# Four transposes of TensorE replaced by one block transpose of VectorE and sixteen transfers within SBUF

## The chip, the cores and the metric

The kernel runs on one core of a Trainium2 chip. A core has TensorE (matmuls and, in a queue of its own, the loads of their weights), VectorE (called DVE in the profile), ScalarE (ACT), GpSimd (POOL), and SyncE (SP), which here only issues transfers. The transfers run on 16 DMA engines. The metric is the device time of one execution in microseconds, the median of some runs.

## The reference, cut to what matters

Four graph layers on x of 128 batches, 128 nodes and 256 features, each followed by a residual sum and a layer norm. The change lies in layer 2, which takes each node's features through three weight matrices and mixes the three results by the diagonal, the upper and the lower triangle of the adjacency matrix:

```python
def _L2_gnn_ref(x, W, adj, bias):
    adj_0 = jnp.diag(jnp.diagonal(adj))
    adj_1 = jnp.triu(adj, k=1)
    adj_2 = jnp.tril(adj, k=-1)
    h = jnp.einsum('bjf,kfo->kbjo', x, W)
    out = jnp.einsum('ij,bjo->bio', adj_0, h[0]) + jnp.einsum('ij,bjo->bio', adj_1, h[1]) + jnp.einsum('ij,bjo->bio', adj_2, h[2])
    return out + bias[None, None, :]
...
# --- layer 2 (adj_resnorm) ---
x = _layernorm(x + _L2_gnn_ref(x, L2_gnn_W, adj, L2_gnn_bias), axis=-1)
```

Layer 1 comes before it: three products with the weights W1, W2, W3, each mixed by the squared adjacency matrix, with a ReLU after the first two. All is float32.

## The kernel before

The 128 batches are handled as 32 quads of four. The loop is a software pipeline: iteration k runs layer 3 of quad a = k - 1, layer 1's end and layer 2 of quad c = k, layer 0's end and layer 1's beginning of quad b = k + 1, the softmax of quad e = k + 2 and the first products of quad g = k + 3. Each engine executes its instructions in the order in which the program writes them.

Many 2 by 2 block products use Strassen and Winograd's seven products instead of eight. The class `Seven` holds them as p1 to p7. Some land in one PSUM bank after each other, so that the intermediate results are read out between them:

```python
def p7(self):
    self.mm(self.y, "S3", "T3", False)
    self.k3 = self.part(self.y, 2)
    self.out(1, 1, self.z, self.k3)

def p4(self):
    self.mm(self.y, "A22", "T4", False)
    self.out(1, 0, self.y, None)

def p3(self):
    self.mm(self.z, "S4", "B22", False)
    self.out(0, 1, self.z, self.k2)
```

In layer 1's first product, `first_seven`, `out` is a sum on VectorE (if something kept is added) and a ReLU on ScalarE, and gives the blocks of h1. `mix2` multiplies the h1 of one node group with the squared adjacency:

```python
def out(row, col, bank, kept_):                    # in first_seven
    h1 = temp("h1")
    if kept_ is not None:
        nc.vector.tensor_add(h1, bank, kept_)
    nc.scalar.activation(h1, bank if kept_ is None else h1, AF.Relu)
    for t in range(2):
        for c in range(2):
            s.h1[2 * row + t, 2 * col + c] = h1[:, (2 * t + c) * P:(2 * t + c + 1) * P]
...
def mix2(k, i):
    pm = ps("pm2").rearrange("p (r c n) -> p r c n", r=2, n=N)
    for c in range(K1):
        nc.tensor.matmul(pm[:, c // 2, c % 2, :], quads[k].h1[i, c], wt_t, start=True, stop=True)
    return pm
```

Layer 2 of quad c is a generator that is advanced step by step between other work. `head(p)` transposes the features of batches 2p and 2p + 1 on TensorE and copies them out of PSUM on ScalarE; `products(p, ...)` forms the sums of a seven-product on VectorE:

```python
def layer2(k, b, room=None):
    s = quads[k]
    adc = adc_tile()
    g = [wk.tile([P, 2, 3 * D], F32, tag="ms", name="g", bufs=1) if room is None else room,
         adc[:, :6 * D].rearrange("p (t f) -> p t f", t=2)]
    ...
    def head(p):
        pt = ps("pt3").rearrange("p (t c n) -> p t c n", t=2, c=DC)
        for t in range(2):
            for c in range(DC):
                nc.tensor.transpose(pt[:, t, c, :], s.xr[:, 2 * p + t, c * P:(c + 1) * P], ident)
        xt = temp("x2t").rearrange("p (t c n) -> p t c n", t=2, c=DC)
        nc.scalar.copy(xt, pt)
        return xt
    ...
    x0 = head(0)
    yield
    u = products(0, x0)
    if b is not None:
        pm = {i: mix2(b, i) for i in (2, 0, 1)}
        x1 = head(1)
        mixed(b, 0, pm[0])
        mixed(b, 1, pm[1])
        pm[3] = mix2(b, 3)
    else:
        x1 = head(1)
    v = products(1, x1)
    ...
    run(u.p1, u.p2, u.p5, u.p6, v.p1, v.p2, u.p7, v.p5, v.p6, u.p4, u.p3, v.p7)
```

The end of an iteration, where the change sits:

```python
        if has_e:
            attention(e)
            scatter(e)                 # four indirect transfers, then the load of the attention weights
        rest = third(c, 2)
        mix1(b, 0)
        mix1(b, 2)
        third_mix(c, 0)
        next(rest)
        w = first_seven(b)
        third_norm(c, 0)               # layer norm of the first two batches of quad c
        next(rest)
        run(w.p1, w.p5, w.p2)
        next(rest)
        if has_g:
            score(g, 0)
            gather_last(g)
        w.p6()
        next(rest, None)
        w.p7()
        third_mix(c, 2)
        w.p4()
        w.p3()
        quads[c].layer2 = layer2(c, b)
        next(quads[c].layer2)          # head(0)
        third_norm(c, 2)               # layer norm of the last two batches of quad c
        next(quads[c].layer2)          # products(0), mix2, head(1), products(1), the products
```

`third_norm` is a square root on ScalarE and the normalisation on VectorE. The tile m2 of quad b, which `mixed` fills for the next product, has seven blocks (B11, B21, B22, T1, T2, T3, T4) of 512 elements a partition; its block T2 is written by `late_sums` at the start of the next iteration.

Of the kernel before, what the change touches and what calls it, by code (L numbers as in the profile page):

```python
# [8 lines left out]
F32 = mybir.dt.float32  # L9
# [17 lines left out]
def gnn_stack(ctx: ExitStack, tc: tile.TileContext, x, adj, w_qv_t, a, w_out_t, src, dst,  # L27
# [18 lines left out]
    P = 128  # L46
# [82 lines left out]
    with ExitStack() as phase:  # L129
# [306 lines left out]
        def scatter(k, load=True):  # L436
            s = quads[k]
            ad = att_dram[k % 2]
            for c in range(NE):
                nc.gpsimd.indirect_dma_start(out=ad, out_offset=bass.IndirectOffsetOnAxis(ap=att_idx[:, c:c + 1], axis=0),  # L440
                                             in_=s.at[:, c, :], in_offset=None)
            if load:
                load_weights(k)
# [54 lines left out]
        def mix1(k, j):  # L498
            s = quads[k]
            pm = ps("pm").rearrange("p (b c n) -> p b c n", b=2, c=DC)  # L500
            for t in range(2):
                for dc in range(DC):
                    nc.tensor.matmul(pm[:, t, dc, :], s.xr[:, j + t, dc * P:(dc + 1) * P], wt_t,
                                     start=True, stop=True)
            mx = temp("mx").rearrange("p (b c n) -> p b c n", b=2, c=DC)
            nc.scalar.copy(mx, pm)
            if j == 0:
                s.mx = {}
                s.h1 = {}
                s.m2 = m2_tile().rearrange("p (t c b n) -> p t c b n", t=7, c=2, b=2)  # L510
            s.mx[j] = mx
# [188 lines left out]
        def third_norm(k, j):  # L700
            s = quads[k]
            xj = s.xr[:, j:j + 2, :]
            norm_apply(wk, xj, s.mv, norm_root(wk, s.mv))
            if j == 0:
                s.xb = wk.tile([P, QB, D], F32, tag="xb", name=f"xb{k}", bufs=1)
            nc.gpsimd.tensor_add(s.xb[:, j:j + 2, :], xj, bias.unsqueeze(1).to_broadcast([P, 2, D]))  # L706

        def layer2(k, b, room=None):

            s = quads[k]
            adc = adc_tile()
            g = [wk.tile([P, 2, 3 * D], F32, tag="ms", name="g", bufs=1) if room is None else room,
                 adc[:, :6 * D].rearrange("p (t f) -> p t f", t=2)]
            sums = [adc[:, 6 * D:], None]
            half = 3 * D // 2
# [11 lines that stand above are left out]
            def products(p, xt):  # L729
                room = sums[p] if p == 0 else temp("x2s")  # L730
                a = {f"A{t + 1}{c + 1}": xt[:, t, c, :] for t in range(2) for c in range(DC)}
                for i in range(4):
                    a[f"S{i + 1}"] = room[:, i * N:(i + 1) * N]
                sums_a(a, a)
                keep = {}

                def mm(bank, i, j, new):
                    nc.tensor.matmul(bank[:, :half], a[i], layer2.blocks[j], start=new, stop=True,  # L738
                                     skip_group_check=True)

                def part(bank, i):
                    if i < 2:
                        keep[i] = temp("x2k")
                    to = keep[i % 2][:, :half]
                    nc.scalar.copy(to, bank[:, :half])  # L745
                    return to

                def out(row, col, bank, kept_):
                    to = g[p][:, row, col * half:(col + 1) * half]
                    if kept_ is None:  # L750
                        nc.scalar.copy(to, bank[:, :half])
                    else:
                        nc.vector.tensor_add(to, bank[:, :half], kept_)

                return Seven(mm, part, out)

            def scaled(p):
                xb = s.xb[:, 2 * p:2 * p + 2, :]
                nc.vector.scalar_tensor_tensor(xb, g[p][:, :, :D], diag_col, xb, op0=ALU.mult, op1=ALU.add)

            def mix(p):
                po = pos[p]
                for i in range(2):
                    nc.tensor.matmul(po, split_t[:, i, :], g[p][:, :, (i + 1) * D:(i + 2) * D],
                                     start=(i == 0), stop=(i == 1))
                return po

            def norm(p, po):
                xj = s.xr[:, 2 * p:2 * p + 2, :]
                nc.vector.tensor_add(xj, s.xb[:, 2 * p:2 * p + 2, :], po)  # L770
                return norm_stats(wk, xj)

            def normed(p, mv):
                norm_apply(wk, s.xr[:, 2 * p:2 * p + 2, :], mv, norm_root(wk, mv))

            x0 = head(0)
            yield
            u = products(0, x0)
            if b is not None:
# [10 lines that stand above are left out]
                mixed(b, 2, pm[2])  # L790
                mixed(b, 3, pm[3])
            run(u.p1, u.p2, u.p5, u.p6, v.p1, v.p2, u.p7, v.p5, v.p6, u.p4, u.p3, v.p7)
            pos = [ps("po2").rearrange("p (t d) -> p t d", d=D) for _ in range(2)]
            yield
            scaled(0)
            v.p4()
            yield
            v.p3()
            po = mix(0)
            scaled(1)  # L800
            yield
            mv = norm(0, po)
            yield
            po = mix(1)
            yield
            normed(0, mv)
            mv = norm(1, po)
            yield
            normed(1, mv)
            nc.sync.dma_start(x3_dram[k], s.xr.rearrange("p b d -> p (b d)"))  # L810
# [112 lines left out]
        def iteration(k):  # L923
# [100 lines left out]
                pass  # L1024
            if has_e:
                attention(e)
                scatter(e)
            rest = third(c, 2)
            mix1(b, 0)
            mix1(b, 2)  # L1030
# [1 line left out]
            next(rest)  # L1032
            w = first_seven(b)
            third_norm(c, 0)
            next(rest)
            run(w.p1, w.p5, w.p2)
            next(rest)
# [14 lines left out]
        def iteration_0():  # L1052

            late_sums(0)
            between = {i: [] for i in range(14)}
            for c, i in ((0, 0), (1, 3), (2, 6)):
                between[i].append(lambda c=c: score(2, c))
            between[2] += [lambda: attention(1), lambda: scatter(1)]
            between[3].append(lambda: gather_last(2))
            second(0, between)  # L1060
            small_loads()
            first_seven.blocks = weight_blocks(w1_sb, w1_s)
            layer2.blocks = weight_blocks(l2w, l2w_s)
            rest = third(0, 0)
            next(rest)
            score(2, NE - 1)
            gather(3)
            for j in range(QB):
                by_row(1, j)
            for _ in rest:  # L1070
                pass
            hidden_sums()
            aggregate(1)
            steps = softmax_parts(2)
            for _ in range(4):
                next(steps)
            stage_a(1)
            third_mix(0, 0)
            rest = third(0, 2)
            next(rest)  # L1080
            third_norm(0, 0)
            next(steps)
            mix1(1, 0)
            next(rest)
            mix1(1, 2)
            w = first_seven(1)
            next(rest)
            w.p1()
            for _ in steps:
                pass  # L1090
            run(w.p5, w.p2)
            next(rest, None)
            attention(2)
            scatter(2)
            w.p6()
            score(3, 0)
            gather_last(3)
            w.p7()
            third_mix(0, 2)
            w.p4()  # L1100
            w.p3()
            quads[0].layer2 = layer2(0, 1)
            next(quads[0].layer2)
            third_norm(0, 2)
            next(quads[0].layer2)
# [565 lines left out]
```

## Time and profile before

| | |
|---|---|
| time, median of 3 runs | 3103.06 us (3100.27 to 3104.02) |
| span of the profiled run | 3097.3 us |
| DMA engines, mean over the span | 109 GB/s of HBM traffic |
| transfers issued by SyncE | 495 |
| transposes of line 724 (`head`) | 256 in 64 calls, 39.6 us busy |

The profile is of one execution. PE is TensorE's matmuls, PEld its weight loads. A group of instructions is named by line, engine, operation, written and read tiles, shape and count; then come the busy time, the mean duration of one, and the idle time of the engine before them with what ended it. A timeline row has start and duration in us, engine, line, operation, tiles, shape and count. Matmuls are pipelined, so that their durations overlap; what one costs the stream is the distance from its start to the next start. L602 and L682 are layer 1's second and third product, L559 is `mix2`, L302 a seven-product of layer 0 or of layer 1's beginning, L738 one of layer 2.

### The profile page before, as it was taken

To read this page: it belongs to the slowest core of one execution; us is meant where nothing else is said; L and a number is where in the kernel's file an instruction comes from. 1 tells how busy PE (TensorE), PEld (TensorE's weight loads), DVE (VectorE), ACT (ScalarE), POOL (GpSimd) and SP (SyncE) were. 2 spreads that over 40 slices of the span, in tenths; PEclk is the share of its full clock that TensorE was granted. 3 is DMA by queue.
4 is the path that set the end of the run, shared out by engine and by line. 5 is a ranking of instruction groups with operands and counts; after the bars stand their busy time and mean duration, and the time that the engine had idled before them with its cause. 6 is when DMAs were issued, how large, how long until landed. Compare 5 with 4: busy or idle time off the path is not lost. (4 is left out here: it accounts for less than half of the span.)

```text
span 3097.3 us, 39721 instructions
## 1 busy us (share of the span) xinstructions
PE 3047.4 (98%) x14576; PEld 2382.0 (77%) x14576; DVE 2311.5 (75%) x4599; ACT 1388.0 (45%) x2547; POOL 652.6 (21%) x536
## 2 busy tenths in 40 slices
PE   8899999999999999999999999999999999999987
PEld 4688888888888888888888888888888887864444
DVE  8777777777777777777777777777777776457888
ACT  3344444344444444443344444444443344326668
POOL 3311112222222121122222211111122220001135
PEclk9999999999999999999999999999999999999999
DMA  5633333334333333333344433333343331015567
GB/s 183 162 103 95 77 97 110 103 103 110 110 103 93 99 103 88 84 103 108 98 110 110 110 96 90 109 95 75 98 110 103 103 110 42 21 44 201 172 206 261
DMA packets 220962, 340.06 MB, mean 110 GB/s; under 512 B 132704, under 2 KB 155104, under 8 KB 212448
## 3 DMA queue, kind: packets, MB, share of 16 engines
q0 software_dynamic: 44688, 148.40, 19.6%
q1 hardware_dynamic: 174320, 188.19, 18.5%
q8 instruction: 116, 1.90, 0.2%
q10 hardware_dynamic: 1760, 0.92, 0.1%
q14 instruction: 78, 0.64, 0.1%
HBM read 252.00 MB, written 85.46 MB: 109 GB/s over the span
## 5 line engine op out<-in xcount | busy, mean ns | idle before, releaser
L602 PE MATMUL ph<-m,w 128*128 128x256 f32 x2048 | 473.1, 379 | 0.0
L682 PE MATMUL p<-w,h 128*128 128x256 f32 x2048 | 462.8, 379 | 0.0
L602 PEld LDWEIGHTS ph<-m,w 128*128 128x128 f32 x2048 | 386.8, 190 | 79.9 <-issue 14.8
L682 PEld LDWEIGHTS p<-w,h 128*128 128x128 f32 x2048 | 388.9, 190 | 66.4 <-issue 7.9
L358 POOL DMA_INDIRECT zs<-qd,src_idx x120 | 116.3, 969 | 1330.2 <-DMA qd<-qt 1295.8
L602 PE MATMUL ph<-m,w_s 128*128 128x256 f32 x1536 | 357.7, 379 | 0.4 <-DVE h L614 0.4
L602 PEld LDWEIGHTS ph<-m,w_s 128*128 128x128 f32 x1536 | 291.7, 190 | 53.7 <-issue 14.8
L358 POOL DMA_INDIRECT zs<-qd,dst_idx x120 | 189.6, 1580 | 339.7 <-DMA zs<-qd,src_idx 330.2
L608 ACT COPY u<-ph 128x512 f32<-128x512 f32 x128 | 74.8, 584 | 354.9 <-PE ph L602 354.9
L440 POOL DMA_INDIRECT attd<-at,att_idx x128 | 142.8, 1116 | 342.3 <-DMA attd<-at,att_idx 251.0
L113 ACT ACTIVATE ln_sd<-ln_mv,eps 128x2 f32<-128x2 f32 x192 | 55.9, 291 | 276.4 <-DVE ln_mv L108 276.3
L618 ACT ACTIVATE h<-h 128x512 f32<-128x512 f32 x192 | 121.1, 631 | 87.2 <-DVE h L614 87.2
L390 DVE SCALAR_TENSOR_TENSOR zs<-zs 128x1024 f32<-128x1024 f32 x125 | 151.3, 1210 | 7.7 <-DMA zs<-qd,dst_idx 5.1
L392 DVE TENSOR_TENSOR zs<-zs,a_bc 128x1024 f32<-128x1024 f32 x125 | 153.2, 1225 | 4.3
L393 DVE TENSOR_REDUCE scores<-zs 128x16 f32<-128x1024 f32 x125 | 152.5, 1220 | 4.3
L745 ACT COPY x2k<-y 128x384 f32<-128x384 f32 x192 | 92.0, 479 | 139.5 <-PE y L738 114.2
L106 DVE BATCH_NORM_STATS2 ln_st<-xr 128x6 f32<-128x256 f32 x384 | 144.5, 418 | 6.6
L121 DVE TENSOR_SCALAR xr<-xr,ln_mv,ln_rs 128x256 f32<-128x256 f32 x384 | 142.5, 413 | 7.0
L459 ACT COPY adc<-ad 128x512 f32<-128x512 f32 x125 | 133.0, 1066 | 7.8 <-DMA ad<-attd 7.8
L706 POOL TENSOR_TENSOR xb<-xr,bias 128x512 f32<-128x512 f32 x64 | 99.1, 1548 | 150.8 <-DVE xr L121 143.7
L559 PE MATMUL pm<-wt_t,h 128*128 128x128 f32 x1024 | 126.8, 277 | 0.0
L559 PEld LDWEIGHTS pm<-wt_t,h 128*128 128x128 f32 x1024 | 121.2, 192 | 1.4 <-issue 1.3
(359 smaller groups left out, 5990.7 us busy)
## 6 DMA issues: line engine op xcount, KB each, us to landing
ad<-attd SPq DMA_DIRECT2D x32, 1024.0 KB, 4.8
zd<-z SPq DMA_DIRECT2D x31, 1024.0 KB, 7.5
zl<-zd SPq DMA_DIRECT2D x62, 512.0 KB, 3.7
xr<-in_x_dram SPq DMA_DIRECT2D x32, 512.0 KB, 7.2
x3d<-xr SPq DMA_DIRECT2D x32, 512.0 KB, 2.6
x3l<-x3d SPq DMA_DIRECT2D x32, 512.0 KB, 4.6
out_dram<-x3l POOLq DMA_DIRECT2D x31, 512.0 KB, 5.0
qd<-qt SPq DMA_DIRECT2D x29, 512.0 KB, 2.6
```

Of the source, the lines that this page charges most:

```text
L106: nc.vector.bn_stats(st[:, i, :], r[:, i, :])
L121: nc.vector.tensor_scalar(r[:, i, :], r[:, i, :], mv[:, i, 0:1], rs[:, i:i + 1], op0=ALU.subtract, op1=ALU.mult)
L358: nc.gpsimd.indirect_dma_start(out=s.z[c], out_offset=None, in_=s.qd, in_offset=bass.IndirectOffsetOnAxis(ap=idx[:, c:c + 1], axis=0), com ...
L390: nc.vector.scalar_tensor_tensor(z, z, SLOPE, z, op0=ALU.mult, op1=ALU.max)
L392: nc.vector.tensor_mul(z3, z3, a_bc.unsqueeze(1).to_broadcast([P, QB, D]))
L393: nc.vector.reduce_sum(s.es[:, c, :], z.rearrange("p (r d) -> p r d", d=DH), axis=AX.X)
L440: nc.gpsimd.indirect_dma_start(out=ad, out_offset=bass.IndirectOffsetOnAxis(ap=att_idx[:, c:c + 1], axis=0), in_=s.at[:, c, :], in_offset= ...
L459: (copy or nc.scalar.copy)(s.adc[:, j * H:(j + 1) * H, :], s.ad.rearrange("p (s r) -> p r s", r=R)[:, j * H:(j + 1) * H, :])
L559: nc.tensor.matmul(pm[:, c // 2, c % 2, :], quads[k].h1[i, c], wt_t, start=True, stop=True)
L602: nc.tensor.matmul(bank[g][:, i].rearrange("p b n -> p (b n)"), wa[:, c, f:f + P], s.m2[:, blk_b, c].rearrange("p b n -> p (b n)"), start= ...
L618: nc.scalar.activation(h, h if src_ is None else src_, AF.Relu)
L682: nc.tensor.matmul(p3[:, t * D:(t + 1) * D], s.h2[f // 2][:, f % 2, j + t, :], w3_sb[:, f, :], start=(f == 0), stop=(f == K2 - 1))
```

## The change

In the first two batches of a quad, and only where layer 2 is interleaved with the following quad (31 of the 32 quads), the transposes leave TensorE. VectorE transposes 128 by 512 elements in blocks of 32 by 32, and sixteen transfers of 32 partitions by four pieces of 32 elements put the blocks into their places, in block T2 of m2, which is free at that time. This starts as soon as the first two batches are normalised. It is meant to free TensorE of four matmuls, and ScalarE of the copy out of PSUM. The load of the attention weights, which waits for the scatters, is moved behind the new transfers on SyncE's queue so that it doesn't hold them up.

```diff
+        def turn_nodes(k, b):
+            s = quads[k]
+            s.g = wk.tile([P, 2, 3 * D], F32, tag="ms", name="g", bufs=1)
+            turned = s.g.rearrange("p t f -> p (t f)")[:, :512]
+            nc.vector.transpose(turned, s.xr[:, :2, :].rearrange("p b d -> p (b d)"))
+            s.x2 = quads[b].m2[:, T2].rearrange("p c b n -> p (c b n)")
+            to = s.x2.rearrange("p (m n) -> p m n", n=N)
+            from_ = turned.rearrange("p (m i a) -> p m i a", i=P // B, a=B)
+            for i in range(P // B):
+                for j in range(N // B):
+                    nc.sync.dma_start(to[i * B:(i + 1) * B, :, j * B:(j + 1) * B], from_[j * B:(j + 1) * B, :, i, :])
+
         def layer2(k, b, room=None):
-            g = [wk.tile([P, 2, 3 * D], F32, tag="ms", name="g", bufs=1) if room is None else room,
+            g = [s.g if room is None else room,
...
-            x0 = head(0)
+            x0 = head(0) if b is None else s.x2.rearrange("p (t c n) -> p t c n", t=2, c=DC)
...
             if has_e:
                 attention(e)
-                scatter(e)
+                scatter(e, False)
...
             third_norm(c, 0)
+            turn_nodes(c, b)
+            if has_e:
+                load_weights(e)
             next(rest)
...
             mix1(1, 2)                     # in the first iteration
+            turn_nodes(0, 1)
             w = first_seven(1)
```

## The prediction

> **What bounds the kernel now.** I read the shares of the engines first (first fence), then the groups of instructions, shapes kept apart (second), then the timeline of one quad from the middle of the run (1400 to 1485 us) engine by engine, because the change sits at one spot of a loop that repeats 31 times.
>
> ```profile
> PE 3047.4 (98%) x14576; PEld 2382.0 (77%) x14576; DVE 2311.5 (75%) x4599; ACT 1388.0 (45%) x2547; POOL 652.6 (21%) x536
> ```
>
> ```profile
> L724 PE MATMUL pt<-ident,xr 128*128 128x128 f32 x256 | 39.6, 277 | 2.0 <-DVE xr L121 2.0
> L726 ACT COPY x2t<-pt 128x512 f32<-128x512 f32 x64 | 36.9, 577 | 47.6 <-PE pt L724 47.6
> L336 DVE STREAM_TRANSPOSE xt<-xg 128x512 f32<-128x512 f32 x56 | 36.2, 685 | 0.0
> ```
>
> TensorE is busy 98% of the span and everything else has room. The chain of waits is of no help here: it ends in the last output after one step. So a gain has to come out of TensorE's own stream, and only if the stream does not stop elsewhere for as long. The quads repeat every 84.78 us (the score transpose of line 407 comes back at that distance nearly everywhere), so what happens in one quad happens about 31 times. TensorE around the spot:
>
> ```profile
> 1428.42 1.03 PE L302 MATMUL z<-w,adc 128*128 128x256 f32 x4
> 1429.28 0.60 PE L724 MATMUL pt<-ident,xr 128*128 128x128 f32 x4
> 1429.72 2.90 PE L559 MATMUL pm<-wt_t,h 128*128 128x128 f32 x24
> 1432.45 0.64 PE L724 MATMUL pt<-ident,xr 128*128 128x128 f32 x4
> 1432.93 1.06 PE L559 MATMUL pm<-wt_t,h 128*128 128x128 f32 x8
> ```
>
> The first L724 row is the work that is removed: `head(0)`. The mean of 277 ns in the group overstates it, since these matmuls are pipelined; the next row starts 1429.72 - 1429.28 = 0.44 us later, so four transposes occupy 0.44 us of the stream. The ceiling of the gain is 31 x 0.44 = 13.6 us, 0.44% of 3103.
>
> Now what the next row waits for. The 24 matmuls of L559 are `mix2` of nodes 2, 0 and 1, eight instructions each. Those of node 0, from its third 128-block on, need the block of h1 that product p3 makes: p3 on TensorE (the 1428.42 row), the sum on VectorE, the ReLU on ScalarE:
>
> ```profile
> 1429.64 0.66 DVE L539 TENSOR_TENSOR h<-z,adc 128x512 f32<-128x512 f32 x1
> ```
>
> ```profile
> 1428.69 0.58 ACT L540 ACTIVATE h<-y 128x512 f32<-128x512 f32 x1
> 1430.33 0.63 ACT L540 ACTIVATE h<-h 128x512 f32<-128x512 f32 x1 [1.05 <-DVE h L539]
> 1430.87 0.57 ACT L726 COPY x2t<-pt 128x512 f32<-128x512 f32 x1
> 1431.33 0.30 ACT L113 ACTIVATE ln_sd<-ln_mv,eps 128x2 f32<-128x2 f32 x1
> ```
>
> In these rows the columns are start, duration, engine, line. The first ScalarE row is p4's ReLU, the second p3's, which ends at 1430.96. The weight loads of TensorE in two short windows:
>
> ```profile
> 1430.73 0.47 PEld L559 LDWEIGHTS pm<-wt_t,h 128*128 128x128 f32 x3
> ```
>
> ```profile
> 1431.01 0.41 PEld L559 LDWEIGHTS pm<-wt_t,h 128*128 128x128 f32 x3
> ```
>
> These loads come every 0.11 us. The three of the first row begin at 1430.73, 1430.84 and 1431.01: the third, which is the first of the second row, is 0.06 late, and it begins 0.05 us after the ReLU's end. It is the thirteenth of the row of 24, the first that needs p3's block. I looked at this load in all 31 quads that have the change: in 30 it begins 0.05 us after the ReLU, and only near 2448 us is it not the last to be ready (0.11). So the stream is already held at this point, by a chain that does not pass through `head(0)`.
>
> **What the skill says.** "VectorE: DVE Perf Modes", section "The three transpose paths", says that VectorE's transpose makes only separate 32 by 32 blocks, a 4 by 4 grid of them, and not one 128 by 128 transpose: hence the transfers that put blocks in place. For its cost I take this trace's 685 ns for the same 128x512 shape. "DMA: Bandwidth & Descriptors", section "Anatomy of one DMA — SWDGE (gpsimd) path", gives a fixed cost of about 2 us for a transfer whatever its size (stated for the other issuing path). The trace agrees: the xg transfers, 64 KB in pieces of 128 B, take a median of 2.3 us from issue to landing. The same page's section "Why small descriptors are slow (HBM only)" says transfers within SBUF are spared the penalty for small pieces; no transfer within SBUF is in this trace. Even pieces that come from HBM with 128 B take 13 ns each here. "TensorE: Matmul & The Clock Gate", section "Measured speedup vs the span model", says matmuls start and end strictly in order; so a wait at one holds all behind it, which the 0.06 us above shows.
>
> **The change, part by part.**
>
> 1. TensorE loses four transposes, 0.44 us per quad. By then `mix2` of node 2 could start at 1429.28 but for p4's ReLU, whose end (1428.69 + 0.58 = 1429.27) plus 0.05 lets it start loading at 1429.32. Twelve loads later, 1429.32 + 12 x 0.112 = 1430.66, the stream stands before the load that needs p3's ReLU, which still ends at 1430.96: p3, its VectorE sum and the ReLU stand where they stood. The load begins at 1431.01, as before. The 0.44 us turn into 0.35 us of waiting there and 0.1 us at the beginning. Gain: 0.
> 2. ScalarE loses one copy of 0.58 us, between that ReLU and the square root of the layer norm. The root moves from 1431.33 to about 1430.9, so VectorE's normalisation ends near 1432.15 instead of 1432.60. `head(1)`, at 1432.45, has its second batch held a little by this (its four transposes take 0.48 us to the next row, not 0.44). Gain: 0.04 us x 30 = 1.2 us. In the first quad `head(1)` stands idle 1.4 us for the same normalisation, behind the same copy: about 0.5 us once.
> 3. VectorE gains one transpose of 0.69 us, after the normalisation that ends at 1419.52. Its next instruction there starts at 1421.65 after 2.13 us of idle time. Hidden, ready at 1420.2.
> 4. Sixteen transfers of 16 KB, each 128 pieces of 128 B, on SyncE's queue, which had nothing to issue between about 1405 and 1427.97. The load_turned transfers (512 pieces each) are issued every 0.53 us (eight in 4.05 us); a single issue of other transfers takes 0.32 to 0.39. I estimate 0.4 us each: 16 x 0.4 = 6.4, last issue near 1426.6, plus 2.3 to land: 1429. With 0.53 us each it is 1431. The ninth must wait for the first, as eight semaphores go round; with 2.3 us to land against 8 x 0.4 = 3.2 that costs nothing. First readers are VectorE's sums, at 1432.1 now, and TensorE at about 1433.8. Hidden with 1 to 3 us to spare. The engines' share: 2048 pieces x 13 ns / 16 = 1.7 us in 8 us in which DMA is a tenth busy.
> 5. The attention weights are loaded behind these: 1427.97 becomes at most about 1429. They landed at 1432.7 and are first used at 1458. Hidden.
> 6. The first reader of the new tile waits on eight DMA semaphores. A wait instruction of TensorE takes 51 ns and names up to two semaphores: some four, 0.2 us. They are handled ahead: in this trace those for the first L738 product stand 0.9 and 0.6 us before its load. I expect 0 to 0.05 us each quad: 0.8 us in all, on average.
>
> Sum: 0 - 1.2 - 0.5 + 0.8, about -1 us: 3102 us.
>
> **The rivals.**
>
> - *The whole 0.44 us is gained*: 3103.1 - 13.6 = 3089.5 us. For it: TensorE is 98% busy, and each removed matmul seems to count. Against it: the load that starts 0.05 us after the ReLU in 30 quads. It holds only if p3's chain also moves, and nothing in it does.
> - *A wait takes the place of the removed work* (my choice): 3099 to 3105 us.
> - *The turned nodes arrive late.* Each microsecond of lateness is up to 31 us: at 2 us late, 3160. For it: gathers still keep DMA 63% busy until about 1421, and 16 fixed costs on one queue are a lot. Against it: 12 us between the transpose and the first reader.
> - *Semaphore waits are not handled ahead*: 0.2 us x 31 = 6 us, 3108 us.
> - *Slower scatters and gathers* through shared DMA engines: VectorE reads the last gathered part at 1455.8, 13 us after it landed, and GpSimd's bias sum ends at 1439.7 and is read at 1448.9. Even 2 us of delay would not reach TensorE: 3102 us.
>
> **Range and chances.** The three runs of before lie 3.8 us apart, so the centre alone carries about 2 us. Downwards a third of the gain could appear (3098); upwards the semaphore waits or a few late quads: 3096 to 3110 us. Over 2% faster, 62 us, is beyond the ceiling of 13.6 us: 0.01. Over 2% slower needs data 2 us late in every quad: 0.02.
>
> **What would show it.** In the changed profile the L559 row of TensorE should begin right after p3's row, and within it a gap of 0.35 us should stand before the thirteenth load, which again begins 0.05 us after the ReLU of L540; p3's row to the first L738 row should stay near 5.4 us. The last of the sixteen issues should land by 1431 on this scale, and VectorE's first sum should wait for no DMA. The prediction is wrong if the quads repeat every 84.3 us (the gain is real), or if TensorE or VectorE waits for the turned tile (later than 85 us).

## The result and the profile after

| | median of 4 runs | range |
|---|---|---|
| before | 3101.87 us | 3100.27 to 3104.02 |
| after | 3142.39 us | 3138.66 to 3146.84 |

The ratio is 1.0131 (95% interval 1.0113 to 1.0148): the change costs 40 us. The quads now repeat every 86.18 us and not every 84.82 (means over 28 quads), and 28 x 1.36 = 38 us.

The shares of the engines in the profile after:

```profile
PE 3057.6 (97%) x14452; PEld 2369.6 (75%) x14452; DVE 2390.3 (76%) x4630; ACT 1369.5 (44%) x2516; POOL 646.2 (21%) x536
```

TensorE has 14576 - 14452 = 124 matmuls less, as intended. VectorE has only 31 instructions more, the new transposes, but is busy 79 us longer. The groups of instructions, shapes kept apart, say where these 79 us are (columns: line, engine, operation, tiles, shapes and count; busy us and mean ns; idle us before, with what ended it):

```profile
L181 DVE TENSOR_TENSOR adc<-m 128x128 f32<-128x128 f32 x31 | 49.5, 1597 | 36.7 <-DMA m<-g 35.7 <-issue 0.8
L182 DVE TENSOR_TENSOR adc<-adc,m 128x128 f32<-128x128 f32 x31 | 23.6, 760 | 1.1
L714 DVE STREAM_TRANSPOSE g<-xr 128x512 f32<-128x512 f32 x31 | 22.1, 712 | 1.1
```

The same first sum in the kernel before, in the same view:

```profile
L181 DVE TENSOR_TENSOR adc<-x2t 128x128 f32<-128x128 f32 x32 | 9.8, 306 | 0.0
```

L181 and L182 are the first two of the four sums that `products(0)` makes of the turned nodes. The first now waits 35.7 us in all for the transfers (`m<-g`), 1.2 us in a quad, and, which is stranger, it *takes* 1597 ns and not 306 for the same 128x128 elements (L182: 760 and not 353). Both come from one spot, here in the quad at 1441 us. Timelines after (start, duration, engine, line), VectorE:

```profile
1441.49 0.71 DVE L714 STREAM_TRANSPOSE g<-xr 128x512 f32<-128x512 f32 x1
...
1453.32 0.74 DVE L121 TENSOR_SCALAR xr<-xr,ln_mv,ln_rs 128x256 f32<-128x256 f32 x2
1455.25 2.67 DVE L181 TENSOR_TENSOR adc<-m 128x128 f32<-128x128 f32 x1 [1.20 <-DMA m<-g]
1457.95 0.29 DVE L182 TENSOR_TENSOR adc<-adc,m 128x128 f32<-128x128 f32 x1
```

SyncE's queue:

```profile
1442.27 10.27 SPq L720 DMA_DIRECT2D m<-g  x16
1452.63 0.54 SPq L449 DMA_DIRECT2D ad<-attd  x1
1453.21 0.43 SPq L205 DMA_DIRECT2D xr<-in_x_dram  x1
```

GpSimd:

```profile
1450.40 1.00 POOL L358 DMA_INDIRECT zs<-qd,src_idx  x1 [0.16 <-issue]
1454.87 1.59 POOL L358 DMA_INDIRECT zs<-qd,dst_idx  x1 [3.48 <-DMA zs<-qd,src_idx]
1455.88 1.88 POOL L706 TENSOR_TENSOR xb<-xr,bias 128x512 f32<-128x512 f32 x1
```

And TensorE:

```profile
1456.37 0.81 PE L752 MATMUL x<-l2w,m 128*128 128x384 f32 x2
1458.06 0.88 PE L752 MATMUL z<-l2w,adc 128*128 128x384 f32 x2 [0.89 <-DVE adc L181]
```

Read them from the transpose's end, at 1442.20.

- SyncE needs 10.27 us for the sixteen issues, 0.64 us each. The last is out 10.3 us after the transpose, and its pieces land at about 12 to 13. VectorE is ready for its sum at 1454.05, 11.85 us after the transpose, and waits 1.20 us.
- The sum then takes 2.67 us. GpSimd's bias sum, 1455.88 + 1.88, ends at 1457.76, and VectorE's sum at 1457.92. In 29 of the 31 quads one of the first two sums is held like this and ends 0.15 to 0.16 us after the bias sum. The sums that follow take 0.28 to 0.29 us again.
- TensorE's product z (u.p5), which needs S1, the first of these sums, starts 1458.06 - 1456.37 = 1.69 us after its neighbour x. Undisturbed, that distance is 0.65 us. In the mean of the quads the distance from one product to the next is longer than before by 0.17 us ahead of the first product, which reads the turned nodes themselves, by 0.45 ahead of z, 0.15 behind z and 0.50 ahead of u.p4: 1.27 of the 1.36 us.

"SBUF — State Buffer", section "🔬 SBUF: two separate sides", says that a VectorE operation with two inputs in SBUF and a GpSimd operation that reads SBUF share a pair of ports under an exclusive lock: one blocks the other for its whole length. The trace agrees that the sum does not end before GpSimd is done. It does not agree in one respect: the record of the sum begins 0.63 us *ahead* of the bias sum's (up to 0.70 ahead in 21 of the 29 quads), so by the page the sum should have held the ports. An indirect transfer of GpSimd is under way at that time, and GpSimd's spans are rough, so I leave the order open.

In the kernel before, in the quad that the prediction shows, GpSimd did this:

```profile
1428.28 0.99 POOL L358 DMA_INDIRECT zs<-qd,src_idx  x1 [0.16 <-DVE h L539]
1437.87 1.88 POOL L706 TENSOR_TENSOR xb<-xr,bias 128x512 f32<-128x512 f32 x1
```

The bias sum stood at 1437.87 to 1439.75, 18 us after the normalisation of the first batches (1419.52), well behind these sums. It stands behind `gather_last` in GpSimd's order: the second L358 row needs the first one's data. Before, the first was issued at 1428.28 and its data landed at 1436.59, behind the attention weights (L449) and the next x (L205). Now those loads stand behind the sixteen transfers, and the gather comes in ahead of them. Counted from the end of the first batches' normalisation, the bias sum starts after 14.4 us (mean of 28 quads) where it used to start after 17.6. So the change delays VectorE's sums and pulls the bias sum forward, until the two meet.

### The profile page after: what moved, and what is told of

Its sections match the earlier page's. It is cut to its first block, busy times and chain, and to the rows that moved or that the text cites. A ratio compares the mean times of both kernels' runs of the same rounds, so it can differ in the third digit from the quotient of the medians.

```text
span 3140.8 us, 40150 instructions
## 1 busy us (share of the span) xinstructions
PE 3057.6 (97%) x14452; PEld 2369.6 (75%) x14452; DVE 2390.3 (76%) x4630; ACT 1369.5 (44%) x2516; POOL 646.2 (21%) x536
## 3 DMA queue, kind: packets, MB, share of 16 engines
q8 instruction: 115, 1.88, 0.2%
## 5 line engine op out<-in xcount | busy, mean ns | idle before, releaser
L358 POOL DMA_INDIRECT zs<-qd,src_idx x120 | 116.3, 969 | 1458.9 <-DMA qd<-qt 1424.0
L358 POOL DMA_INDIRECT zs<-qd,dst_idx x120 | 188.0, 1567 | 249.2 <-DMA zs<-qd,src_idx 241.5
L559 PE MATMUL pm<-wt_t,h 128*128 128x128 f32 x1024 | 136.5, 282 | 2.6
```

The source lines that it names most:

```text
L358: nc.gpsimd.indirect_dma_start(out=s.z[c], out_offset=None, in_=s.qd, in_offset=bass.IndirectOffsetOnAxis(ap=idx[:, c:c + 1], axis=0), com ...
```

## The experiments

Two theories stood after this view. *Lateness*: the transfers land too late, and each microsecond of it goes into the quad. *Overlap*: the data would be nearly in time, but VectorE's sums are held under GpSimd's bias sum. A third question is step 1 of the prediction: does TensorE gain nothing by losing the transposes, because `mix2` waits for p3's ReLU?

### No transfers: e1 and e2

`e1` leaves the sixteen transfers out and reads VectorE's blocks as they lie, so what it computes is not the reference's. `e2` also moves the two `mix2` that do not need p3's ReLU ahead of it.

```diff
 # e1
+            s.direct = turned
-            for i in range(P // B):
-                for j in range(N // B):
-                    nc.sync.dma_start(to[...], from_[...])
-            x0 = ... s.x2.rearrange(...)
+            x0 = ... s.direct.rearrange(...)
 # e2: e1 and
-                pm = {i: mix2(b, i) for i in (2, 0, 1)}
+                pm = {i: mix2(b, i) for i in (2, 3, 0)}
                 x1 = head(1)
                 mixed(b, 0, pm[0])
+                pm[1] = mix2(b, 1)
                 mixed(b, 1, pm[1])
-                pm[3] = mix2(b, 3)
```

> Leaves out the sixteen transfers: VectorE transposes blocks, and layer 2 reads them where VectorE left them, so the nodes of the first two batches are not fully transposed. Late-data theory (the turned tile arrives after its first reader is ready, and that is the whole loss): the loss goes, 3098 to 3104 us, VectorE's first sum waits for no DMA, and TensorE still stands about 0.35 us before the thirteenth load of mix2, because the ReLU of p3 holds it. Rival 'removed matmuls count': 3089 us. Rival 'the added VectorE work or the moved load of the weights costs': above 3115 us.

> As e1, and mix2 takes the nodes in the order 2, 3, 0, then head(1), then 1, so that sixteen instead of eight loads that need nothing of p3 stand before the first that does. ReLU theory: TensorE no longer stands there, the 0.44 us of the four transposes and the 0.06 us of before come free, about 0.5 us x 31 = 15 us: 3086 to 3092 us. Rival (the stop only moves to another wait, such as head(1) for VectorE's normalisation): 3097 us or more.

Measured: e1 3095.55 us, 0.9981 of before (0.9973 to 0.9990), with a quad of 84.78 us; e2 3084.19 us, 0.9942 (0.9925 to 0.9958), with a quad of 84.43 us. Both lie about 2 us below the ranges that I expected. So without transfers the four transposes are worth next to nothing in a quad (84.82 before), and with the order changed 0.39 us. The waiting can be seen in the changed kernel itself. TensorE's weight loads in two short windows of its profile, the first ending where the second begins:

```profile
1452.14 0.53 PEld L559 LDWEIGHTS pm<-wt_t,h 128*128 128x128 f32 x4
```

```profile
1452.95 0.74 PEld L559 LDWEIGHTS pm<-wt_t,h 128*128 128x128 f32 x6 [0.28 <-ACT h L540]
```

and ScalarE's ReLU of p3 in its timeline:

```profile
1452.27 0.63 ACT L540 ACTIVATE h<-h 128x512 f32<-128x512 f32 x1 [1.06 <-DVE h L539]
```

The ReLU ends at 1452.90, and the thirteenth load begins 0.05 us later, as in the kernel before. Beyond the usual 0.11 us from load to load, the hole ahead of it is now 0.35 us a quad (mean), where it was 0.06. Of the 6 us by which e1 is faster, its quads hold about 1 (28 x 0.04) and the last phase of the kernel 2, to which I come below. The rest is not in the profiles, whose two executions lie only 2.2 us apart.

### The reordering alone: e6

The same reordering in the kernel before, which still has its transposes.

> The kernel before with mix2 in the order 2, 3, 0, head(1), 1 and nothing else. ReLU theory: only the 0.06 us of before are to be had, 0.06 x 31 = 2 us: 3098 to 3102 us. Rival (the reordering alone brings what e2 brought, 17 us): 3084 us.

Measured: 3101.09 us, 0.9997 (0.9988 to 1.0006). Alone it is worth nothing, since `head(0)` fills the time until the ReLU. The e2 gain needs both: the transposes gone, and something else to do for TensorE.

### Transfers that nobody waits for: e3

The sixteen transfers run, but the sums read VectorE's blocks (so e3, too, computes something else).

```diff
+            s.direct = turned
-            x0 = ... s.x2.rearrange(...)
+            x0 = ... s.direct.rearrange(...)
```

> All sixteen transfers run as in the changed kernel, but layer 2 reads the blocks where VectorE left them and waits for no transfer (nodes not fully transposed). Late-data theory: as e1, within 5 us. Rival 'shared DMA engines' (the transfers slow the scatters, gathers and loads that others wait for): above 3115 us, with longer waits for gathers or weights.

Measured: 3105.21 us, 1.001 (1.0001 to 1.0018), with a quad of 84.84 us. The transfers' own traffic and their issues cost the quad nothing. It is 9.7 us slower than e1, where I had expected at most 5: the last phase of the kernel takes 7 us more than in e1 (below), the quads 2. The 40 us come from reading what the transfers bring. That leaves both theories standing: without the wait the sums are also early, and out of the bias sum's way.

e1 and e3 also show what pulls the bias sum forward. Both have the load of the attention weights moved. In e1, where no transfers stand ahead of it, the bias sum starts 17.0 us after the normalisation, nearly as before (17.6); in e3, with the transfers, 14.7. So it is not the move alone but the sixteen transfers, which hold that load and the next x back.

### The gather later: e4, and its control e10

`gather_last` behind layer 2's products, in the changed kernel (e4) and in the kernel before (e10).

```diff
                 score(g, 0)
-                gather_last(g)
             w.p6()
...
             next(quads[c].layer2)
+            if has_g:
+                gather_last(g)
```

> The changed kernel with the gather of the last part (gather_last, all but in the first iteration) moved behind the issue of layer 2's products, so its 4 KB pieces no longer meet the last of the sixteen transfers. If the gather makes the tail late (issues end 9.7 us after the transpose, pieces last until 11.2 to 13.2): most of the loss goes, 3103 to 3118 us, VectorE's wait at its first sum falls from 1.2 us to under 0.5. If the issue rate alone makes it late: unchanged, 3135 us or more. A third way: the gather now comes too late for its score, and VectorE waits there.

> Control for e4: the kernel before with the gather of the last part moved as in e4. If the gather's place matters only to the sixteen transfers: 3099 to 3104 us. Rival (moving it gains by itself, and e4 merely sums a loss and a gain): 3090 us or less.

Measured: e4 3100.88 us, 0.9996 (0.9987 to 1.0004); e10 3098.75 us, 0.9988 (0.9981 to 0.9995). The first sum in e4, from the groups of instructions:

```profile
L181 DVE TENSOR_TENSOR adc<-m 128x128 f32<-128x128 f32 x31 | 18.5, 598 | 11.8 <-DMA m<-g 7.9 <-issue 3.7
```

The whole loss is gone, and I first read it as "the gather's 4 KB pieces delayed the transfers". That reading fell: the line shows the wait for data down from 35.7 to 7.9 us, but the sum's duration down as well, from 1597 to 598 ns. With the gather out of the way, GpSimd makes its bias sum already 11.9 to 13.2 us after the transpose. The overlap is still there, in 26 of the 31 quads, but it is over earlier: the four sums end 14.0 us after the transpose (mean) and not 16.1, and TensorE's distances are the undisturbed ones. The edit changes both suspects at once. In e10 the same move gains 3 us without any transfers.

In e4 nothing stands just ahead of the bias sum on GpSimd, and there the one that starts first is not held: in the quad at 1421 us a sum that starts at 1433.79, 0.16 us ahead of the bias sum, takes 0.28 us, and the next, 0.16 behind it, takes 1.28 and ends 0.15 us after it.

### The bias sum alone, later: f1

This parts the two theories. Only GpSimd's bias sum moves, behind the last of VectorE's eight sums for layer 2; a copy of one column that reads that sum holds it there. Everything else, gather and transfers, stays.

```diff
-            third_norm(c, 2)
+            third_norm(c, 2, False)           # without the bias sum
             next(quads[c].layer2)
+            third_bias(c, 2, quads[c].last_sum)
...
+                nc.gpsimd.tensor_copy(late, after[:, 0:1])    # after = the last sum
             nc.gpsimd.tensor_add(s.xb[:, j:j + 2, :], xj, bias...)
```

> The changed kernel with one thing moved: GpSimd's bias sum of the last two batches waits for the last of VectorE's eight sums (a one-column copy on GpSimd that reads it), so the two engines no longer work on it at once. Transfers, gather and load stay, so VectorE waits for the data as before (1.2 us on average). Collision theory (the late data hurts because it pushes VectorE's sums under the bias sum, where one of them takes up to 2.7 us instead of 0.28): 3095 to 3108 us. Late-data theory (the wait itself costs): 3128 us or more.

Measured: 3106.55 us, 1.0018 (1.0009 to 1.0027), with a quad of 85.01 us. The group of the first sum (its line is 182 in this kernel):

```profile
L182 DVE TENSOR_TENSOR adc<-m 128x128 f32<-128x128 f32 x31 | 9.1, 293 | 44.5 <-DMA m<-g 38.4 <-issue 6.1
```

One quad on VectorE:

```profile
1441.02 0.29 DVE L182 TENSOR_TENSOR adc<-m 128x128 f32<-128x128 f32 x1 [1.43 <-DMA m<-g]
```

on GpSimd:

```profile
1440.66 1.58 POOL L359 DMA_INDIRECT zs<-qd,dst_idx  x1 [3.94 <-DMA zs<-qd,src_idx]
1444.30 0.18 POOL L714 COPY late<-x2s 128x1 f32<-128x1 f32 x1 [2.06 <-DVE x2s L185]
1444.45 1.27 POOL L715 TENSOR_TENSOR xb<-xr,bias 128x512 f32<-128x512 f32 x1
```

and on TensorE:

```profile
1441.90 0.81 PE L762 MATMUL x<-l2w,m 128*128 128x384 f32 x2
1442.55 0.81 PE L762 MATMUL z<-l2w,adc 128*128 128x384 f32 x2
```

The wait for the data is even longer than in the changed kernel (44.5 us of idle time in all, 36.7 there). Still most of the loss is gone, because each sum takes 293 ns again and z follows x by 0.65 us: against the kernel before, measured beside each, the changed one loses 40.5 us and f1 5.6. So the overlap is the cause of about 35 of the 40 us. The lateness by itself costs the rest: in 10 quads TensorE's first product, which reads the turned nodes themselves, waits for the transfers, 0.23 us a quad on average, 28 x 0.23 = 6 us. And the gather's indirect transfer is not what holds the sums: here it runs at 1440.66 to 1442.24, across the sum at 1441.02, which takes its usual 0.29 us. But the lateness is what brings the sums to where the bias sum stands; either cure takes most of the loss away.

### Longer pieces and other shapes: e5, e11

Why did sixteen issues take 10.3 us and not the estimated 6.4? Two guesses: the 128 pieces of 128 B (or the 32 partitions) make an issue slow, or any issue behind another takes this long. `e5` moves the same bytes in pieces of 512 B, to other places, so its output differs:

```diff
-                    nc.sync.dma_start(to[i * B:(i + 1) * B, :, j * B:(j + 1) * B], from_[j * B:(j + 1) * B, :, i, :])
+                    nc.sync.dma_start(s.x2[i * B:(i + 1) * B, j * N:(j + 1) * N], turned[j * B:(j + 1) * B, i * N:(i + 1) * N])
```

`e11` issues four of each of four shapes back to back, 16 KB each, and nobody reads them (the sums read VectorE's blocks, as in e3):

```diff
-            for i in range(P // B):
-                for j in range(N // B): ...
+            for j in range(4): ...    # 32 partitions x 4 pieces of 128 B
+            for j in range(4): ...    # 128 partitions x 1 piece of 128 B
+            for j in range(4): ...    # 32 partitions x 1 piece of 512 B
+            for j in range(4): ...    # 64 partitions x 1 piece of 256 B
```

> The changed kernel with the same sixteen transfers of 16 KB, but of 32 pieces of 512 B each instead of 128 of 128 B (the blocks land in wrong places: the block order of the free dimension is not turned). If the 0.645 us from issue to issue come from the number of pieces: about 0.4 us or less, VectorE does not wait, 3098 to 3108 us. If they come with each transfer within SBUF whatever its pieces (my choice, as 512 pieces from HBM are issued every 0.53 us): 0.6 us or more and 3130 to 3145 us.

> A look at issue times alone: sixteen transfers of 16 KB within SBUF that nobody waits for, four each of 32 partitions x 4 pieces of 128 B (as in the change), 128 partitions x 128 B, 32 partitions x 512 B, 64 partitions x 256 B; layer 2 reads the blocks where VectorE left them (nodes not fully transposed). If any transfer within SBUF costs SyncE 0.6 us: all four alike. If it is the number of partitions that a transfer touches: near 0.6 with 32, 0.5 with 64, 0.35 with 128. If pieces: 128 pieces (first and second shape) slower than 64 and 32. Time near e3: 3095 to 3108 us.

Measured: e5 3135.89 us, 1.0105 (1.0088 to 1.0121), its issues 0.63 us apart. e11 3104.9 us, one run. The instructions of its four source lines, with least, median and greatest duration in ns:

```profile
L721 SPq DMA_DIRECT2D m<-g x124: 591/608/899, 143.3 to 2687.3; - x124
L723 SPq DMA_DIRECT2D g<-g x124: 465/599/1402, 146.0 to 2689.9; - x124
L725 SPq DMA_DIRECT2D g<-g x124: 507/589/1572, 148.6 to 2692.4; - x124
L727 SPq DMA_DIRECT2D g<-g x124: 585/594/1487, 151.8 to 2695.0; - x124
```

Neither guess holds. For the four shapes an issue costs SyncE about 0.6 us alike, so it is not the pieces or the partitions. It is not the row either: in the changed kernel SyncE has issued nothing for 17 us when the first of the sixteen comes, and that one takes as long as the others (a window that holds it alone; its median over the quads is 0.60 us too):

```profile
1442.27 0.60 SPq L720 DMA_DIRECT2D m<-g  x1
```

So it goes mostly with the transfer: 0.6 us for each of these within SBUF, 0.49 for an xg transfer from HBM of 512 pieces. What is ahead can add to it: the load of the attention weights took 0.32 us before and takes 0.54 right behind the sixteen. The reason for the 0.6 us these runs don't show. Fewer transfers, not longer pieces, are the remedy.

### Five transfers through HBM: e7 and e8

The transposed tile goes to HBM in one transfer and comes back in four, which put the blocks in place. `e8` has e2's reordering as well.

```diff
+            there = turn_dram[k % 2]
+            nc.sync.dma_start(there, turned)
+            back = there.rearrange("(j q) (m i a) -> i q m j a", q=B, i=P // B, a=B)
+            to = s.x2.rearrange("p (m j a) -> p m j a", j=N // B, a=B)
             for i in range(P // B):
-                for j in range(N // B): ...
+                nc.sync.dma_start(to[i * B:(i + 1) * B], back[i])
```

> As e8 but with mix2 in its old order: the only difference from the changed kernel is that five transfers through HBM take the place of sixteen within SBUF, the gather stays where it was. Late-data theory: no wait at VectorE's first sum, the ReLU of p3 holds TensorE as in e1: 3096 to 3104 us. Rival (the gather alone makes any transfer late, however early issued): above 3110 us.

> Five transfers instead of sixteen: the transposed blocks are written to HBM in one transfer of 256 KB and read back by four of 64 KB that put them in place; mix2 reordered as in e2; gather where it was. Estimate: one issue, 2.6 us to land, four issues of 0.53 us, 2.3 us to land: 7.3 us after the transpose, before the gather's pieces come at 8 us and before VectorE is ready at 11.9 us. If the lateness of the data is the loss: as e2, 3082 to 3092 us. Rival (the two fixed costs and the gather make it late again): above 3100 us.

Measured: e7 3097.19 us, 0.9982 (0.9973 to 0.9990); e8 3089.90 us, 0.9958 (0.9941 to 0.9974), with a quad of 84.41 us. SyncE in e8:

```profile
1415.83 0.32 SPq L718 DMA_DIRECT2D turnd<-g  x1
1417.88 2.61 SPq L722 DMA_DIRECT2D m<-turnd  x4
```

and VectorE:

```profile
1415.09 0.71 DVE L715 STREAM_TRANSPOSE g<-xr 128x512 f32<-128x512 f32 x1
...
1427.57 0.28 DVE L182 TENSOR_TENSOR adc<-m 128x128 f32<-128x128 f32 x1
```

The last issue is over 4.7 us after the transpose, not 10.3, and the first sum neither waits nor is stretched. The data is moved twice, but the queue is occupied for less time.

### The other cures: e9, f4, f5 and f6

`e9` is e4 with e2's reordering; `f4` is f1 and e4 together; `f5` is f1 with the reordering; `f6` is all three.

```diff
 # f4: third_norm(c, 2, False), third_bias(c, 2, ...) of f1; gather_last(g) where e4 has it
 # e9, f5, f6: e4, f1, f4 and
-                pm = {i: mix2(b, i) for i in (2, 0, 1)}
+                pm = {i: mix2(b, i) for i in (2, 3, 0)}    # and so on, as in e2
```

> The changed kernel with the gather moved as in e4 and mix2 reordered as in e2. ReLU theory: e4's 3100.9 less the 0.45 to 0.5 us x 31 = 14 to 15 us: 3084 to 3092 us; but since mix2's reordering makes TensorE reach layer 2's products 0.45 us earlier while VectorE's wait for the data (0.36 us in e4) stays, part of it may be lost: up to 3097 us. Rival (with sixteen transfers the data is late by as much as TensorE gains): 3100 us.

> As f1, and the gather behind the bias sum, so that its pieces do not meet the transfers either. Collision theory: as f1, the data's remaining lateness being hidden, 3094 to 3104 us. Late-data theory: as e4 (3101 us) and well below f1.

> f1 with mix2 reordered as in e2. Collision theory: TensorE reaches the product that reads the first sum about 14.4 us after the transpose, the data lets the sum end at 13.4 on average and 14.9 at most: most of the 0.45 us is gained, 3084 to 3096 us. Late-data theory: 3115 us or more.

> f4 with mix2 reordered: nothing left in TensorE's way in either theory, 3083 to 3091 us. If it is no faster than e9 (3090 us), the bias sum's place is worth nothing once the gather is out of the way.

| | median us | ratio to before (95%) | quad us |
|---|---|---|---|
| e9 | 3090.03 | 0.9962 (0.9948 to 0.9976) | 84.40 |
| f4 | 3101.66 | 1.0002 (0.9993 to 1.0011) | 84.75 |
| f5 | 3099.43 | 0.9992 (0.9984 to 1.0001) | 84.69 |
| f6 | 3090.55 | 0.9966 (0.9954 to 0.9978) | 84.41 |

f5 missed: I had reckoned with the product that reads the first sum, but the first product of layer 2 reads the turned nodes themselves, and as in f1 TensorE waits there, in 11 quads, 0.25 us a quad on average. f6, with the gather out of the way too, hardly does (0.01 us). e8, e9 and f6 are equally good, 0.4% faster than the kernel before and 1.7% faster than the changed one (3090 / 3142.4), and 6 us above e2, which has no transfers.

### The weights' load left in front: e12

The change moved the attention weights' load behind the transfers. What if it stays where it was?

```diff
-                scatter(e, False)
+                scatter(e)                 # with the load
...
             turn_nodes(c, b)
-            if has_e:
-                load_weights(e)
```

> The changed kernel without the move of the load of the attention weights: in SyncE's queue it stands ahead of the sixteen transfers again and holds them until the scatters have landed, some 7 us later. Late-data theory (each microsecond of lateness costs TensorE about one): VectorE waits 8 to 9 us at its first sum, 31 x 7 = 220 us more than the changed kernel: 3330 to 3400 us. Rival (the late data is only a small part of what costs): below 3250 us.

Measured: 3412.54 us, 1.099 (1.097 to 1.101), with a quad of 96.11 us, somewhat above what I had expected. The load stands on SyncE's queue until the scatters are through, and the sixteen transfers stand behind it. TensorE's timeline:

```profile
1605.62 1.62 PE L752 MATMUL y<-l2w,m 128*128 128x384 f32 x2 [8.31 <-DMA m<-g]
1607.03 1.49 PE L752 MATMUL x<-l2w,m 128*128 128x384 f32 x2
1608.31 1.49 PE L752 MATMUL z<-l2w,adc 128*128 128x384 f32 x2
1609.59 1.00 PE L752 MATMUL y<-l2w_s,adc 128*128 128x384 f32 x2
1610.42 0.81 PE L752 MATMUL y<-l2w,x2t 128*128 128x384 f32 x2
```

The move was needed, then. The mean quad pays 11.3 us for 9.1 us of added idle time. In the quad shown, with 8.3 us of it, the products behind it start 1.41, 1.28, 1.28 and 0.83 us apart and not 0.65, another 2.2 us. "TensorE: Matmul & The Clock Gate", section "What's actually happening", says that an idle TensorE drops to half its clock and needs a few microseconds of work to get it back. These rows agree: half the rate for 1609.59 - 1605.62 = 4 us, and the profile's record of the granted clock is 0.5 from 1599.7 to 1610.0 us.

### What stays open

The last phase of the kernel, which writes the outputs (from the first of the products with `diag`, L1569 in the kernel before, to the end), took 112.6 us before, 117.6 after, 117.5 in e3, 115.3 in e8, 116.0 in f4, and 110.6, 109.2 and 112.2 in e1, e2 and e6. I found no rule in it; with up to 8 us it is the whole difference between kernels whose quads are alike (e3 and before, or e8 and e2). No run was made for it. Open too is why VectorE's sum is held although its record begins ahead of the bias sum's, and why an issue within SBUF takes 0.6 us. Not tried: spreading the sixteen issues over several engines' queues, so that two or more issue side by side.

## Why the prediction was wrong, step by step

1. *TensorE's four transposes turn into waiting.* Right: the hole before the thirteenth load is 0.35 us, as expected, and e1's quad is 84.78 us. e2 and e6 show its other half, that an order which fills the hole is worth 0.39 us a quad.
2. *The copy's removal gains 1 to 2 us.* e1's quad gains 0.04 us, as worked out. It is drowned in the rest.
3. *VectorE's transpose is hidden.* Right: 712 ns each, and e3 loses nothing in the quad.
4. *Sixteen issues of 0.4 us, 6.4 us.* This is the term that was mis-sized: 0.645 us each, 10.3 us. I scaled down from the 0.53 us of issues with 512 pieces, as if the number of pieces made the price, and took single issues of other transfers for the lower bound. e5 and e11 show that the pieces don't make it, and the first of the sixteen shows that the row doesn't either. The last pieces land 11.2 to 13.4 us after the transpose, not 9, and the margin of "1 to 3 us" was used up: VectorE waits 1.2 us.
5. *The attention weights' load moves, hidden.* For its own reader it is. But it was looked at from that reader only. The step that failed is the last rival, "even 2 us of delay would not reach TensorE": it asked what a *later* bias sum would do, and no part asked what an *earlier* one would do. With the load and the next x held back by the sixteen transfers (e1 against e3) the gather landed sooner, and the bias sum came 3 us earlier, onto the sums that step 4's error had pushed back. f1 shows that this is 35 of the 40 us.
6. *Semaphore waits cost 0 to 0.05 us.* Right: in f4, where the data is hardly late, the first product starts 0.11 us after the matmul ahead of it, as in the kernel before.

The rival "the turned nodes arrive late, 2 us late makes 3160" named the right direction and too high a price for lateness: f1 has 1.4 us of waiting in each quad, 44 us in all, and loses 5.6. VectorE waits in nearly every quad, but TensorE still has `mix2` to do before it needs the turned nodes and two products more before it needs a sum; it waited in 10 quads only. What the rival left out is that a late sum can meet another engine's work.

## What to carry to other kernels

Count the transfers that follow each other on one queue, and price them at what an issue of that kind costs there, before counting bytes and pieces. The sixteen here occupied SyncE for 10.3 us, and the DMA engines by my estimate for 1.7 (2048 pieces of 13 ns on 16 engines). When a change moves a transfer or delays an engine, lay the timelines of VectorE and GpSimd over each other at that spot, in both directions: an instruction that comes earlier can do as much harm as one that comes later. A group whose mean duration rises without a change of shape, as L181 here, is a sign of a collision; look which other engine's instruction ends at the same time, and move that one alone to be sure.

## What was unexpected of the hardware

- Issues on SyncE of transfers within SBUF: 0.59 to 0.61 us each (medians), for four shapes of 16 KB from 32 partitions x 4 pieces to 128 partitions x 1 piece, and 0.60 for the first one on an idle queue. e8's first transfer, 256 KB from SBUF to HBM, took 0.32.
- A VectorE sum of two SBUF tiles of 128x128, normally 0.28 us, took up to 2.73 us and a median of 1.95 us in the changed kernel, ending 0.16 us after GpSimd's 128x512 sum.
- After 8.3 us of idle time, TensorE made its next three pairs of 128x384 products at half the rate, over 4 us.
